# Inverse transform in four array quadrants, with a new order of pieces, in a spectral mixture-of-experts kernel

## The chip, the cores and the metric

The kernel runs on one core of a Trainium2 chip. The core has a matrix engine (TensorE, "PE" in the profile; its weight loads are shown as "PEld"), three engines for elementwise work (VectorE "DVE", ScalarE "ACT", GpSimd "POOL"), and a queue engine (SyncE "SP") that issues most transfers. TensorE writes into PSUM, an accumulator memory of eight banks; ACT and DVE move results from there to the on-chip memory SBUF. The metric is the device time of one execution in microseconds (us).

## The reference

The input x has 16 images of 64 channels and 128 x 128 pixels; all is float32. Two layers follow each other. The first:

```python
x_ht = dht_2d(x)                                   # 2-D Hartley transform
out_ht = zeros.at[:, :, :20, :20].set(compl_mul2d(x_ht[:, :, :20, :20], w1))
y = dht_2d(out_ht) / (H * W)
y = gaussian_smoothing_4d(y)                       # over all four axes
return y * (jnp.abs(fftfreq(W)) <= 0.25)           # only 65 of 128 columns stay
```

The second, on the result x of the first:

```python
residual = x
h = _afno(_group_norm(x, gn1_w, gn1_b), ...)       # 32 x 32 modes: MLP, inverse FFT
h = h + residual
residual = h
feats = _gelu(_c1(_group_norm(h, gn2_w, gn2_b), fe_w, fe_b))
shared = sum(_gelu(_c1(feats, shared_w[s], shared_b[s])) / 2 for s in range(2))
# gate: feats.mean -> small MLP -> scores of 16 experts; top 4, softmax
out = shared + sum(_gelu(_c1(feats, expert_w[e], expert_b[e])) * gate_w[:, e] for e in range(16))
return out + residual
```

An image is therefore the sum of two low-rank parts in the spectral domain, brought to pixels (one from the 32 x 32 modes of the second layer, one from the 20 x 20 modes of the first, the residual), then a channel mixing, then two shared and four chosen experts.

## The kernel before

**Three stages.** The first (lines up to 266) loads all of x and transforms it to 400 modes per image; the blur over images is folded into the sums `x2`. Between it and the second comes the modes stage (L288 to L321): 11 steps over `k1`, each of 40 fp32 matmul instructions into a PSUM tile `ps` that several copies take apart into `om` (ACT and DVE both on each tile), and a small product with `blurc` into `ot`. The second stage (L370 to L556) finds the group-norm statistics of the images from their modes, and runs the first MLP layer on 32 x 32 spectral points of each image (`spec` is its table of 3.2 MB); results go to device memory (`o1d`, and the 20 x 20 modes as `od` and `ond`).

**The mixture stage** (from L568) works on one image after the other, 16 in all, in pieces of fixed shape, each with a PSUM tile `pe` of two banks out of three such tiles:

- `spectrum` (L602): loads by the SP queue of the MLP values `s` and of the 20 x 20 modes into columns 64 and up of `bm`.
- `spectrum_f` (L613), two pieces: second MLP layer, 64 matmuls each, and one ACT copy (L629) into columns 0 to 63 of `bm`.
- `rows` (L635), eight tiles: transform along one image axis. Four matmuls per channel pair of 128 columns, in the four 64 x 64 quadrants of TensorE's array; ACT copies 105 partitions into `u` (L652). Partitions 0 to 63 of `u` hold the part of the 32 x 32 modes, 64 to 104 the residual's, and two more (105, 106) a bias term that `prepare` makes in the second stage and that reaches `u` through device memory (`b2x`).
- `pixels` (L658), eight tiles: the transform along the other axis, eight matmuls of 107 x 128 by 128 columns (both parts and the bias in one contraction). ACT evacuates with a bias into an `h` tile (L677), and DVE takes its statistics (L681, two per tile).
- `norm` (three steps), `feature` (eight tiles; L732, ACT's gelu L736) and `gate` (eight small steps, with four indirect loads of the chosen experts' weights on POOL, L806).
- `group`, 48 of them: an expert on a tile; four quadrant matmuls (L826), a gelu on ACT into one of the `g` tiles (L831), a weighted add into `h` on DVE (L834). The last expert of a tile is followed by its store.

A float32 matmul of the source is two instructions of TensorE, each with a weight load. On each engine instructions run in the order that was built. ACT evacuations are written one piece behind (`on_act`), DVE adds and statistics one more behind (`on_dve`).

**The order** of the pieces is written out by hand in `PIECES`: each piece has a list of positions, counted in groups of its own image (48 per image). Negative positions count back from the image's own group 0, so pieces of later images lie among the groups of the current one: -50 is two groups before group 0 of the image before it. Pieces are sorted by position, then by their place in the list.

Of the kernel before, what the change touches and what calls it, by code (L numbers as in the profile page):

```python
# [19 lines left out]
K = 20  # L20
# [10 lines left out]
KU = KC + 2  # L31
# [23 lines left out]
def constant_tables():  # L55
# [23 lines left out]
    inv1, inv2 = np.zeros((128, 2, N)), np.zeros((KU, N))  # L79
# [7 lines left out]
    inv2[KC], inv2[KC + 1] = inv2[:32].sum(0), inv2[32:64].sum(0)  # L87
    c, s = np.cos(a32).sum(0), np.sin(a32).sum(0)
    bias = np.array([[c, s], [-s, c]])

    by_half = lambda t: t.reshape(-1, 2, 2, N // 2).transpose(0, 1, 3, 2).reshape(-1, 2 * N)
    inv1, bias = by_half(inv1), by_half(bias)
# [38 lines left out]
    for loc in range(5):  # L131
# [13 lines left out]
        "bias": bias,  # L145
# [14 lines left out]
def hartley_afno_moe_kernel(ctx: ExitStack, tc: tile.TileContext, a: dict, out: bass.AP):  # L160
# [26 lines left out]
    with tc.tile_pool(name="modes", bufs=1) as mp:  # L187
# [6 lines left out]
        with tc.tile_pool(name="f_x", bufs=10) as xp, tc.tile_pool(name="f_t", bufs=2) as tp, \  # L194
# [9 lines left out]
            def along_columns(b, t1):  # L204
# [20 lines left out]
                for bo in range(NB):  # L225
                    g = float(gb[bo, b])
                    if g == 0.0:
                        continue
                    to = x2[:, 0, bo, :]
                    if bo in seen:  # L230
                        nc.vector.scalar_tensor_tensor(to, xf, g, to, ALU.mult, ALU.add)
                    else:
                        nc.vector.tensor_scalar(to, xf, g, None, ALU.mult)
                        seen.add(bo)
                    if not gb[bo, b + 1:].any():
                        nc.scalar.mul(x2[0:C, 1, bo], x2[C:P, 0, bo], -1.0)
                        nc.scalar.copy(x2[C:P, 1, bo], x2[0:C, 0, bo])
# [39 lines left out]
        spec = load(sc, "spec", [CH, 4, 2 * MD * MD])  # L277
        exw = load(sc, "exw", [P, C, NE])

        with tc.tile_pool(name="m_o", bufs=1) as op, \  # L280
# [7 lines left out]
            for k1 in range(K // 2 + 1):  # L288
# [9 lines left out]
                nc.scalar.copy(lok[:, k1], lo[:, :, 0])  # L298
                nc.vector.tensor_copy(upk[:, k1], up[:, :, 0])
                if k1 % (K // 2):  # L300
                    nc.scalar.copy(lok[:, K - k1, 0:1], lo[:, 0:1, 1])
                    nc.scalar.copy(lok[:, K - k1, K // 2 - 1:0:-1], lo[:, 1:, 1])
                    nc.vector.tensor_copy(upk[:, K - k1, ::-1], up[:, :, 1])
# [18 lines left out]


# [10 lines left out]
    b2 = kp.tile([2, C], F32, name="b2t")  # L334
    for ri in range(2):
        nc.sync.dma_start(b2[ri:ri + 1], a["b2"][32 * ri:32 * ri + 1, 0:C])
    bias = load(kp, "bias", [2, 2, N])
    b2r = kp.tile([P, 2, C], F32, name="b2r")
    b2x = dram.tile([2, N, C], F32, name="b2x")
    inv1 = load(kp, "inv1", [P, 2, N])  # L340
    inv2 = load(kp, "inv2", [KU, N])
# [20 lines left out]
    bm = kp.tile([P, CL, KC], F32, name="bm")  # L362
# [8 lines left out]
    with tc.tile_pool(name="s_w", bufs=2) as sw, tc.tile_pool(name="s_o", bufs=1) as so, \  # L371
# [134 lines left out]
        def prepare():  # L506
# [8 lines left out]
            ps = pp3.tile([P, 512], F32, name="pso")  # L515
            for i in range(2):
                nc.tensor.matmul(ps[:, i * C:(i + 1) * C], lhsT=bias[:, i], rhs=b2, start=True, stop=True)
            nc.scalar.copy(b2r.rearrange("p i c -> p (i c)"), ps[:, 0:2 * C])
            nc.sync.dma_start(b2x.rearrange("i n c -> n i c"), b2r)
# [50 lines left out]
    with s3:  # L570
        up_, hpp, fp, gp, selp = (pool(n, q) for n, q in (
            ("u", 1), ("hp", 14), ("feats", 9), ("g", 7), ("selw", 2)))
# [5 lines left out]
        nc.sync.dma_start(u[KC:KU], b2x)  # L578
# [22 lines left out]

        def spectrum(box):  # L602

            b = box["b"]
            s = box["s"] = sp.tile([P, MD * MD], F32, name="s")
            nc.sync.dma_start(s, o1d[b].rearrange("r c k -> (r c) k"))
            for h in range(2):
                r, i = (0, 32) if h else (64, 96)
# [4 lines left out]
        def spectrum_f(box, q):  # L613
# [13 lines left out]
            def evacuate():  # L627
                bmf = bm[:, :, 0:64].rearrange("p c (r j) -> p r c j", r=2)
                nc.scalar.copy(bmf[:, :, :, q * 16:(q + 1) * 16], ps.rearrange("p i r c -> p r c i"))  # L629
# [5 lines left out]
        def rows(box, q):  # L635


            if q == 0:
                if "spectrum" not in box:
                    flush()  # L640
            ps = ps2.tile([P, 2, 4, N], F32, name="pe")
            for i in range(4):
                for part, h in ((0, 0), (1, 0), (0, 1), (1, 1)):
                    k0 = C * (h ^ part)
                    rs = slice(k0, k0 + (HR if part else C))
                    cs = slice(64, KC) if part else slice(0, 64)
                    nc.tensor.matmul(ps[cs, h, i, :], lhsT=bm[rs, 4 * q + i, cs],  # L647
                                     rhs=inv1[rs, part], start=True, stop=True)

            def evacuate():  # L650
                dst = u[0:KC].rearrange("p n (h s) -> p h s n", h=2)[:, :, 4 * q:4 * q + 4, :]
                nc.scalar.copy(dst.rearrange("p h s n -> p n h s"),  # L652
                               ps[0:KC].rearrange("p h s n -> p n h s"))
# [4 lines left out]
        def pixels(box, t):  # L658
# [8 lines left out]
            for r in range(8):  # L667
                row = t * 8 + r
                nc.tensor.matmul(  # L669
                    ps[:, r // 4, r % 4 * N:(r % 4 + 1) * N],  # L670
                    lhsT=u[0:KU, 2 * row:2 * row + 2, :].rearrange("p h c -> p (h c)"),
                    rhs=inv2, start=True, stop=True)
# [190 lines left out]
        def step(name, make):  # L863
# [9 lines left out]
            (lambda box, i: spectrum(box), (-84,)),  # L873
            (spectrum_f, (-57, -50)),
            (feature, (-5, -4, -3, -2, -2, -2, -2, 0)),
            (step("norm", norm2), (-19, -16, -10)),
            (step("gate", gate), (2, 3, 5, 7, 8, 8, 10, 12)),
            (rows, (-50, -49, -48, -48, -48, -40, -39, -38)),
            (pixels, (-36, -32, -28, -24, -24, -24, -23, -23)),
# [80 lines left out]
```

## Time and profile before

| | us |
|---|---|
| median of 5 runs | 1856.02 (1853.68 to 1860.78) |
| the profiled execution | 1854.06 |
| its span, first to last instruction | 1852.0 |
| PE busy | 1696.2 (92%) |
| ACT busy | 1377.4 (74%) |
| DVE busy | 1270.6 (69%) |

By stage: the first takes 266 us and is filled by the load of x (the DMA engines are 90% and more busy until 200 us), the modes stage ends at 294 us, the second stage at 477 us, the first group starts at 532 us, and the mixture stage then repeats every 83 to 85 us. A "busy" TensorE counts matmuls with modelled ends, so 92% is not the share of its peak. In the lines, "<-" after an idle time names what ended it, and "issue" means that nothing in the profile did.

### The profile page before, as it was taken

The numbers are of one execution on the slowest core, as the hardware profiler recorded it, in microseconds if no ns is written. First come the engines' busy times: TensorE is split into PE (matmuls) and PEld (weight loads), VectorE is DVE, ScalarE is ACT, GpSimd is POOL, SyncE is SP. The second block draws the span as 40 slices with busy tenths as digits, with TensorE's granted clock in tenths as the row PEclk, the third lists the DMA queues.
The fourth block names the chain that finished last, engine by engine and source line by source line (L and its number), as shares of the span: only waits on it lengthen the run. The fifth ranks groups of instructions, "written<-read, shape, count | busy, mean of one in ns | idle before, by whom it ended". The sixth has DMA issues, their size and how long they took to land. (4 is left out here: it accounts for less than half of the span.)

```text
span 1852.0 us, 55817 instructions
## 1 busy us (share of the span) xinstructions
PE 1696.2 (92%) x24644; PEld 937.6 (51%) x24644; DVE 1270.6 (69%) x1774; ACT 1377.4 (74%) x1690; POOL 120.7 (7%) x140
## 2 busy tenths in 40 slices
PE   6677768999889999999999999999999999999996
PEld 5677764333645555454545455454545455554521
DVE  1233332322249788797979797887979797887988
ACT  2334343112478999989898989989898999989897
POOL 0000002003010101010110101010100101010110
PEclk9989989999999999999999999999999999999998
DMA  9989842114212222322232322322232322222023
GB/s 337 317 304 329 284 138 67 59 58 137 58 25 61 57 81 44 97 36 81 47 79 50 70 81 36 92 49 81 36 85 55 70 70 48 70 58 70 27 71 92
DMA packets 136129, 181.00 MB, mean 98 GB/s; under 512 B 94201, under 2 KB 95414, under 8 KB 135658
## 3 DMA queue, kind: packets, MB, share of 16 engines
q1 hardware_dynamic: 132192, 171.73, 33.0%
q0 software_dynamic: 3696, 5.71, 1.2%
q8 instruction: 193, 3.16, 0.7%
q14 instruction: 48, 0.39, 0.1%
HBM read 98.29 MB, written 79.11 MB: 96 GB/s over the span
## 5 line engine op out<-in xcount | busy, mean ns | idle before, releaser
L834 DVE SCALAR_TENSOR_TENSOR h<-g,wt,h 128x1024 f32<-128x1024 f32 x512 | 620.8, 1275 | 86.0 <-ACT g L831 86.0
L831 ACT ACTIVATE g<-pe,wl 128x1024 f32<-128x1024 f32 x512 | 540.0, 1128 | 9.4 <-PE pe L826 7.9
L826 PE MATMUL pe<-f,wl 64*64 64x512 f32 x4096 | 496.1, 600 | 2.1 <-DMA wl<-exd,ati 0.3
L834 DVE SCALAR_TENSOR_TENSOR h<-g,h 128x1024 f32<-128x1024 f32 x256 | 301.5, 1220 | 56.1 <-ACT g L831 56.1
L831 ACT ACTIVATE g<-pe,vec_sb 128x1024 f32<-128x1024 f32 x256 | 278.0, 1134 | 20.2 <-PE pe L826 20.1
L669 PEld LDWEIGHTS pe<-inv_sb,u 107*128 107x128 f32 x2048 | 234.4, 192 | 65.9 <-ACT g L831 35.1
L826 PEld LDWEIGHTS pe<-f,wl 64*64 64x64 f32 x4096 | 136.0, 132 | 238.5 <-ACT g L831 99.0
L669 PE MATMUL pe<-inv_sb,u 107*128 107x128 f32 x2048 | 248.8, 279 | 4.1 <-ACT g L831 2.8
L826 PE MATMUL pe<-f,shw 64*64 64x512 f32 x2048 | 251.2, 600 | 0.0
L677 ACT ACTIVATE h<-pe,gs 128x1024 f32<-128x1024 f32 x128 | 142.4, 1114 | 73.5 <-PE pe L669 61.3
L250 PE MATMUL ps<-fwd_sb,xt 128*64 128x64 f32 x4096 | 144.2, 234 | 56.3 <-issue 49.4
L681 DVE BATCH_NORM_STATS2 stats<-h 128x6 f32<-128x512 f32 x256 | 160.3, 679 | 27.1 <-ACT h L677 26.9
L250 PEld LDWEIGHTS ps<-fwd_sb,xt 128*64 128x64 f32 x4096 | 139.0, 150 | 59.8 <-issue 52.5
L647 PE MATMUL pe<-inv_sb,bm 64*64 64x128 f32 (+1 forms) x4096 | 143.4, 273 | 2.5 <-issue 2.5
L736 ACT ACTIVATE f<-pe,fb 128x1024 f32<-128x1024 f32 x128 | 144.1, 1136 | 1.7 <-PE pe L732 1.7
L253 ACT COPY t<-ps 128x320 f32<-128x320 f32 x128 | 53.3, 426 | 123.0 <-PE ps L250 122.8
L647 PEld LDWEIGHTS pe<-inv_sb,bm 64*64 64x64 f32 (+1 forms) x4096 | 117.0, 123 | 49.7 <-ACT f L736 24.5
L732 PE MATMUL pe<-h,fs 64*64 64x512 f32 x1024 | 133.1, 607 | 1.6 <-DVE n L709 1.6
L652 ACT COPY u<-pe 105x1024 f32<-105x1024 f32 x128 | 127.2, 1042 | 4.2 <-PE pe L647 3.2
L219 DVE TENSOR_TENSOR xm<-ps,pn 64x20 f32<-64x20 f32 x32 | 5.5, 171 | 177.4 <-ACT pn L215 177.2
L548 PE MATMUL psx<-spec_sb,ot 100*64 100x512 f32 x512 | 115.6, 594 | 0.0
L806 POOL DMA_INDIRECT wl<-exd,ati x64 | 66.8, 1044 | 696.8 <-ACT g L831 604.5
(164 smaller groups left out, 1153.7 us busy)
## 6 DMA issues: line engine op xcount, KB each, us to landing
xt<-in_x_dram SPq DMA_DIRECT2D x128, 512.0 KB
out_dram<-h SPq DMA_DIRECT2D x256, 256.0 KB
o1d<-o SPq DMA_DIRECT2D x16, 512.0 KB
s<-o1d SPq DMA_DIRECT2D x16, 512.0 KB
bm<-od SPq DMA_DIRECT2D x96, 50.0 KB
wk<-in_w_dram SPq DMA_DIRECT2D x11, 320.0 KB
wn<-in_w_dram SPq DMA_DIRECT2D x11, 320.0 KB
spec_sb<-in_spec_dram SPq DMA_DIRECT2D x1, 3200.0 KB
```

The lines of the kernel that those rows point to most:

```text
L250: nc.tensor.matmul(ps[cols, i, :], lhsT=xt[:, i, cols], rhs=fwd1, start=True, stop=True)
L548: nc.tensor.matmul(ps[ri * C:(ri + 1) * C], lhsT=ot[:, kc, b * C:(b + 1) * C], rhs=spec[:, kc, ri * 1024 + n * 512:ri * 1024 + (n + 1) * 512],
L647: nc.tensor.matmul(ps[cs, h, i, :], lhsT=bm[rs, 4 * q + i, cs], rhs=inv1[rs, part], start=True, stop=True)
L652: nc.scalar.copy(dst.rearrange("p h s n -> p n h s"), ps[0:KC].rearrange("p h s n -> p n h s"))
L669: nc.tensor.matmul(ps[:, r // 4, r % 4 * N:(r % 4 + 1) * N], lhsT=u[0:KU, 2 * row:2 * row + 2, :].rearrange("p h c -> p (h c)"), rhs=inv2, ...
L677: nc.scalar.activation(h, ps, AF.Identity, bias=gs1[:, 1, box["b"]:box["b"] + 1])
L681: nc.vector.bn_stats(box["stats"][:, 2 * t + p, :], h[:, p])
L732: nc.tensor.matmul(ps[p * C:(p + 1) * C, half], lhsT=box["fs"][rows_], rhs=box["h"][t][rows_, p], start=True, stop=True)
L736: nc.scalar.activation(f, ps, AF.Gelu, bias=box["fb"], accum_out=box["sums"][:, t:t + 1])
L826: nc.tensor.matmul(ps[half * C:(half + 1) * C, p], lhsT=w[rows_], rhs=f[rows_, half], start=True, stop=True)
L831: nc.scalar.activation(g, ps, AF.Gelu, bias=bias)
L834: nc.vector.scalar_tensor_tensor(h, g, share(), h, ALU.mult, ALU.add)
```

## The change

- Rows: each tile is 64 matmuls of 64 columns instead of 32 of 128, each quadrant filled. In `u`, partitions 0 to 63 are now one half of the pixels of an axis and 64 to 127 the other; the two parts (32 x 32 modes, residual) lie behind each other in columns.
- Pixels: per four image rows, four quadrant matmuls of 128 columns for the one part, then four that add the other part on the 66 columns that can be other than zero.
- The bias is no longer made in `prepare` and sent through device memory; it is added in the evacuation of `spectrum_f`, which is now two DVE operations of 512 elements a partition each instead of one ACT copy.
- `spectrum` is split: the load of `s` (`spectrum_in`) at -90, the loads of the modes at -74. The first `spectrum_f` piece is at -77 (behind the pixels of the image before), the second stays at -50. Rows, pixels, norm steps, features and gate steps have new positions.
- 16 instead of 14 `h` buffers, 8 instead of 7 `g` buffers; `bm` has 128 columns instead of 105.
- First stage: one of the two `x2` copies of an image is on DVE. Modes stage: all copies of a tile are on one engine, ACT and DVE in turn. The loads of `spec` and `exw` come after the modes stage.

```diff
-                        nc.scalar.copy(x2[C:P, 1, bo], x2[0:C, 0, bo])
+                        nc.vector.tensor_copy(x2[C:P, 1, bo], x2[0:C, 0, bo])
...
-        spec = load(sc, "spec", [CH, 4, 2 * MD * MD])
-        exw = load(sc, "exw", [P, C, NE])
...
-                nc.scalar.copy(lok[:, k1], lo[:, :, 0])
-                nc.vector.tensor_copy(upk[:, k1], up[:, :, 0])
+                copy = nc.vector.tensor_copy if k1 % 2 else nc.scalar.copy
+                copy(lok[:, k1], lo[:, :, 0])
+                copy(upk[:, k1], up[:, :, 0])
                 if k1 % (K // 2):
-                    nc.scalar.copy(lok[:, K - k1, 0:1], lo[:, 0:1, 1])
-                    nc.scalar.copy(lok[:, K - k1, K // 2 - 1:0:-1], lo[:, 1:, 1])
-                    nc.vector.tensor_copy(upk[:, K - k1, ::-1], up[:, :, 1])
+                    copy(lok[:, K - k1, 0:1], lo[:, 0:1, 1])
+                    copy(lok[:, K - k1, K // 2 - 1:0:-1], lo[:, 1:, 1])
+                    copy(upk[:, K - k1, ::-1], up[:, :, 1])
...
+    sc2 = on_modes.enter_context(tc.tile_pool(name="s_c2", bufs=1, side="right"))
+    spec = load(sc2, "spec", [CH, 4, 2 * MD * MD])
+    exw = load(sc2, "exw", [P, C, NE])
...
-            ps = pp3.tile([P, 512], F32, name="pso")
-            for i in range(2):
-                nc.tensor.matmul(ps[:, i * C:(i + 1) * C], lhsT=bias[:, i], rhs=b2, start=True, stop=True)
-            nc.scalar.copy(b2r.rearrange("p i c -> p (i c)"), ps[:, 0:2 * C])
-            nc.sync.dma_start(b2x.rearrange("i n c -> n i c"), b2r)
+            for r0 in (32, 96):
+                nc.scalar.mul(b2[r0:r0 + 32, 1], b2[r0:r0 + 32, 1], -1.0)
...
-            ("u", 1), ("hp", 14), ("feats", 9), ("g", 7), ("selw", 2)))
+            ("u", 1), ("hp", 16), ("feats", 9), ("g", 8), ("selw", 2)))
...
-        nc.sync.dma_start(u[KC:KU], b2x)
...
+        def spectrum_in(box):
+            s = box["s"] = sp.tile([P, MD * MD], F32, name="s")
+            nc.sync.dma_start(s, o1d[box["b"]].rearrange("r c k -> (r c) k"))
+
         def spectrum(box):
 
             b = box["b"]
-            s = box["s"] = sp.tile([P, MD * MD], F32, name="s")
-            nc.sync.dma_start(s, o1d[b].rearrange("r c k -> (r c) k"))
...
-                nc.scalar.copy(bmf[:, :, :, q * 16:(q + 1) * 16], ps.rearrange("p i r c -> p r c i"))
+                for i in (0, 8):
+                    j = q * 16 + i
+                    nc.vector.tensor_tensor(bmf[:, :, :, j:j + 8],
+                                            ps[:, i:i + 8].rearrange("p i r c -> p r c i"),
+                                            b2.unsqueeze(3).to_broadcast([P, 2, CL, 8]), ALU.add)
...
-            ps = ps2.tile([P, 2, 4, N], F32, name="pe")
+            ps = ps2.tile([P, 2, 4, 2, C], F32, name="pe")
             for i in range(4):
-                for part, h in ((0, 0), (1, 0), (0, 1), (1, 1)):
-                    k0 = C * (h ^ part)
-                    rs = slice(k0, k0 + (HR if part else C))
-                    cs = slice(64, KC) if part else slice(0, 64)
-                    nc.tensor.matmul(ps[cs, h, i, :], lhsT=bm[rs, 4 * q + i, cs],
-                                     rhs=inv1[rs, part], start=True, stop=True)
+                for part in range(2):
+                    for h, p in ((0, 0), (1, 1), (1, 0), (0, 1)):
+                        rs = slice(h * C, h * C + (HR if part else C))
+                        nc.tensor.matmul(ps[p * C:(p + 1) * C, h, i, part, :],
+                                         lhsT=bm[rs, 4 * q + i, part * C:(part + 1) * C],
+                                         rhs=inv1[rs, part, p * C:(p + 1) * C], start=True, stop=True)
...
-            for r in range(8):
-                row = t * 8 + r
-                nc.tensor.matmul(
-                    ps[:, r // 4, r % 4 * N:(r % 4 + 1) * N],
-                    lhsT=u[0:KU, 2 * row:2 * row + 2, :].rearrange("p h c -> p (h c)"),
-                    rhs=inv2, start=True, stop=True)
+            quadrants = ((0, 0), (1, 1), (0, 1), (1, 0))
+            for r in range(4):
+                n = 2 * (4 * t + r)
+                for p, half in quadrants:
+                    k = slice(p * C, (p + 1) * C)
+                    nc.tensor.matmul(ps[half * C:(half + 1) * C, p, r * N:(r + 1) * N],
+                                     lhsT=u[k, n + half, :], rhs=inv2[k, 0:N], start=True, stop=False)
+                for p, half in quadrants:
+                    k = slice(p * C, (p + 1) * C)
+                    to = ps[half * C:(half + 1) * C, p, r * N:(r + 1) * N]
+                    nc.tensor.matmul(bass.AP(to.tensor, to.offset, [to.ap[0], (N - MH, 2), (1, MH)]),
+                                     lhsT=u[k, C + n + half, :],
+                                     rhs=inv2[k, N:].rearrange("k (a n) -> k a n", a=2),
+                                     start=False, stop=True)
...
-            (lambda box, i: spectrum(box), (-84,)),
-            (spectrum_f, (-57, -50)),
-            (feature, (-5, -4, -3, -2, -2, -2, -2, 0)),
-            (step("norm", norm2), (-19, -16, -10)),
-            (step("gate", gate), (2, 3, 5, 7, 8, 8, 10, 12)),
-            (rows, (-50, -49, -48, -48, -48, -40, -39, -38)),
-            (pixels, (-36, -32, -28, -24, -24, -24, -23, -23)),
+            (lambda box, i: spectrum_in(box), (-90,)),
+            (lambda box, i: spectrum(box), (-74,)),
+            (spectrum_f, (-77, -50)),
+            (feature, (-8, -8, -4, -3, -3, -3, -3, -1)),
+            (step("norm", norm2), (-24, -21, -16)),
+            (step("gate", gate), (2, 3, 4, 5, 6, 7, 9, 11)),
+            (rows, (-48, -47, -45, -44, -43, -40, -39, -39)),
+            (pixels, (-34, -34, -33, -32, -31, -30, -30, -28)),
             (group, range(NG)),
```

## The prediction

> **What bounds the kernel now.** The page first: TensorE is busy for 92% of the span, and its code comes in 193 fetches: 3.16 MB for two instructions per matmul, so 64 bytes each and 256 to a fetch.
>
> ```profile
> span 1852.0 us, 55817 instructions
> PE 1696.2 (92%) x24644; PEld 937.6 (51%) x24644; DVE 1270.6 (69%) x1774; ACT 1377.4 (74%) x1690; POOL 120.7 (7%) x140
> q8 instruction: 193, 3.16, 0.7%
> ```
>
> Then busy times by window over one image of the mixture stage (gate to gate 83.3 to 84.9 us, mean 83.75). The columns are the stretch, then PE, PEld, DVE, ACT, POOL.
>
> ```profile
> 1031.50:1052.00 20.50, 19.09 (x308) 9.55 (x308) 14.82 (x24) 19.66 (x25) 0.32 (x1) 1.00 0.18 53
> 1052.00:1081.00 29.00, 28.76 (x248) 18.60 (x244) 27.17 (x33) 24.15 (x24) 4.66 (x5) 1.00 0.34 56
> 1081.00:1115.50 34.50, 33.74 (x562) 14.15 (x554) 28.35 (x33) 33.48 (x41) 0.56 (x1) 1.00 0.28 79
> ```
>
> ACT has almost no idle time in the first and third window, and 4.9 us in the second, that of the pixels: there it waits for TensorE. The timeline of TensorE shows the pace:
>
> ```profile
> 1069.77 5.63 PE L669 MATMUL pe<-inv_sb,u 107*128 107x128 f32 x48
> 1075.33 1.09 PE L826 MATMUL pe<-f,wl 64*64 64x512 f32 x8
> 1076.35 3.84 PE L669 MATMUL pe<-inv_sb,u 107*128 107x128 f32 x32
> ```
>
> and that of ACT in the same stretch, with the idle time and who ended it in brackets:
>
> ```profile
> 1073.65 1.11 ACT L677 ACTIVATE h<-pe,gs 128x1024 f32<-128x1024 f32 x1 [0.67 <-PE pe L669]
> 1075.43 1.11 ACT L677 ACTIVATE h<-pe,gs 128x1024 f32<-128x1024 f32 x1 [0.67 <-PE pe L669]
> ```
>
> A pixel tile takes 1.78 us (16 matmuls 0.1115 apart), a change between the 128x128 and the 64x64 mode 0.15 to 0.2 each way (1075.33 to 1076.35 is 1.02 for a group that takes 0.87 among others); ACT needs 1.00 for either. So ACT bounds most of the image, TensorE the pixels. VectorE is idle 13.4 us an image.
>
> Groups by line price the new parts (engine, operation, tiles, count | busy, mean ns | idle before), and two lines of TensorE's timeline at the first image show a wait with no engine behind it:
>
> ```profile
> L652 ACT COPY u<-pe 105x1024 f32<-105x1024 f32 x128 | 127.2, 1042 | 4.2 <-PE pe L647 3.2
> L629 ACT COPY bm<-pe 128x1024 f32<-128x1024 f32 x32 | 33.7, 1054 | 13.6 <-PE pe L622 13.3
> L483 DVE TENSOR_TENSOR ok<-psd,st 128x512 f32<-128x512 f32 x10 | 12.2, 1221 | 12.3 <-PE psd L480 12.3
> L681 DVE BATCH_NORM_STATS2 stats<-h 128x6 f32<-128x512 f32 x256 | 160.3, 679 | 27.1 <-ACT h L677 26.9
> ```
>
> ```profile
> 481.83 0.22 PE L622 MATMUL pe<-v2b,s 128*32 128x64 f32 x1 [1.57 <-issue]
> 488.23 0.52 PE L647 MATMUL pe<-inv_sb,bm 64*64 64x128 f32 x9 [1.28 <-issue]
> ```
>
> The last two are 256 TensorE instructions apart and follow no semaphore. 1.4 us before each, a packet of the code queue ended, and these packets never start closer than 3.3 us in the trace. I read: a block of 256 instructions can't be used up in less than some 3.4 us.
>
> **The change part by part.** Per image, in start-to-start times.
>
> *Pixels.* A tile becomes 64 matmuls in four quadrants: four rows, each of two sets 128 wide and two 66 wide. Sets 128 wide run 0.109 apart in the rows stage (L647, four quadrants at once). For 66 wide no row exists: pairs 64 wide (L212) start 0.0584 apart, so 0.060; the upper bound is 0.109, if a weight load or the strided output holds them to the wider pace. Tile: 4 x (0.219 + 0.120) = 1.36, with ramp 1.40 (bound 1.80). No mode change is left.
>
> *Rows.* 64 matmuls of 64 columns instead of 32 of 128: 16 sets x 0.0584 = 0.93 for 0.88 now. ACT's 0.92 per tile stays (same 1024 elements a partition), and ACT bounds there: nothing. If that cover went, 8 x 0.05 = 0.4.
>
> *Evacuating the spectrum.* ACT loses 2 x 1.05 = 2.1. VectorE gets four tensor_tensor of 512. Bounds 0.69 (L440, same size, contiguous) and 1.22 (L483, scattered output); runs of eight lie between: 0.95, so 3.8 of its 13.4 idle. Behind them on VectorE are adds and statistics, for which ACT waits only when the eight g buffers are full: from the end of a g to the start of its add the lag grows to 4.5 us before the features today; later to perhaps 7, of 8 x 1.15 = 9. What it can cost is the PSUM buffer, one of three, held until VectorE comes, and rows that wait for bm; behind the features the lag is near 0 (10 us idle there today), and two groups and a feature lie between.
>
> *Order.* The pixels move from 14 groups to 7 (groups 14 to 20, with a spectrum piece). TensorE there: 8 x 1.40 + 7 x 0.87 + 2.2 for the piece (1.92 and mode changes) = 19.5. Code: 8 x 128 + 256 + 112 = 1392 instructions, 5.4 blocks, 18.5 us at 3.4: mostly hidden, but two tiles, a group and the piece in a row are 528 instructions in 5.9 us, where 7 are needed: 1.0. Less 0.5 that TensorE is ahead of ACT at its start: 20.0. ACT has 15 us of work there: 5.0 idle, for 6.2 today (28.2 us from group 11 to 25 for 22 of work).
> The second spectrum piece, among the features: ACT had its own copy (1.05) to fill TensorE's 2 us; now it idles 1.0. So half of the 2.1 comes back as a wait. Norm steps come 4, 3 and 5 groups after what they need (4, 3 and 6 now) and wait on VectorE's lag: 0.9 (1.0 now). Features come 8 groups after the last norm step instead of 5; the eighth still waits for group 46 to free its f buffer. Gate steps stand one group and mostly one row apart, where two groups or none stood; ACT's work lies between either way: 0. Rows behind the second piece, code: 0.4.
> ACT work 48 x 1.00 + 8 x (0.92 + 1.00 + 1.09) + 2.35 (gate, its waits, norm) = 74.4; with idle 5.0 + 1.0 + 0.9 + 0.4 the period is 81.7, so -2.05. Fifteen images' stretches: -31. Bounds: stretch 18 (no code stall) to 23.2 (66-wide sets at 0.109): -4.1 to +1.2 each, -62 to +18.
>
> *Queues.* SP: the s load and eight spectrum loads go from group 12 to 6 and 22; they land within 6.5 us and are needed 13 and 26 groups later. The store and load through b2x go, and two small matmuls and a copy in `prepare`, off the path; so does a 64 KB load ahead of the first pixels. POOL: gathers one group earlier, used from group 16; its memset of bm grows by a fifth, unawaited. hp with 16 buffers ends ACT's wait for stores (7.5 us in all, inside the stretches counted).
>
> *First image.* Two pieces, eight rows, eight pixels without groups, so code bounds: rows 8 x 1.7 = 13.6 for 10.6, pixels 13.6 for 14.5, a piece among them +1.4, two VectorE evacuations +0.4, other waits -1.4: +2.5 (-5 to +6).
>
> *Modes stage.* 27.8 us for 11 steps. Today ACT and VectorE take turns on one tile (four copies of 0.41 to 0.46, a small one, 0.53 idle at each turn: 2.05 a step), and TensorE twice stood 3 us beside the load of spec. Then whole tiles alternate: (1.2 + 1.85 + 0.4) / 2 = 1.7 a step, 19.8 in all: -8. The spec load (23 us) starts after it and lands some 8 us before its first use; its effect on code fetches moves with it to a stretch where TensorE is busy 30.3 of 31.2: +4. Net -4 (-11 to +4).
> *x2 copies.* The last five pairs on ACT (0.54 each) split over two engines: -1.3 (-2.7 to +1).
>
> Sum, against the profiled execution's 1854.06: -31 + 2.5 - 4 - 1.3 = 1820. That execution lies 2 us under the median of the runs: 1822.
>
> **A rule weighed.** The Trainium skill (Runtime: NRT & Kernel Launch, Instruction fetch mechanics) says that TensorE holds 2048 instructions and that crossing a block of 256 is mostly hidden. The idle 1.57 and 1.28 us above say otherwise. By the page the 1.4 us a period and 8 in the first image would go: some 1793.
>
> **The rivals.**
> *Code bounds (slower).* TensorE's instructions per image go from 2300 to 3500. Before 488.23 a fetch came 3 us late beside a 512 KB load. The pixel stretch has 5.4 blocks; it reaches today's share of idle time at 22 us, so at 4.1 us a block. At 4.5 it takes 24.3, 4.3 more than forecast: 81.7 + 4.3 = 86.0, 2.3 above today's, 15 x 2.3 + 5 for the first image = 40 over 1856: 1895. Against: steady-state packets take 1.0 us, and loads were put apart from the dense places.
> *Quadrants slow (slower).* 66-wide sets at 0.109: 3.2 more than forecast each period, 1822 + 48 = 1870. Against: pairs of L212 load 64 columns each in 0.0584.
> *VectorE's lag sets the norm steps (no change).* Evacuations at 1.22 and the pixels' statistics bunched put the lag near 4 at the first norm step; it and the next then wait 1 us each: +1.9 a period on the forecast, 1850. For: today a norm step already waits 1.1 us on it.
> *Fetch hidden.* The change gives all its TensorE time: 1793.
>
> **How the numbers follow.** Forecast (1803 to 1843) 0.46; fetch hidden 0.20; VectorE's lag 0.12; code bounds 0.15; quadrants slow 0.07. A difference under 0.2% (3.7 us) can't be told from none. Faster 0.46 + 0.20 + half of 0.12 = 0.72; same 0.05; slower 0.23. The range leaves out most of code-bound and the best of hidden fetch: 1783 to 1869.
>
> **What would show it.** Pixel tiles 1.35 to 1.45 us apart where two follow each other; ACT idle near 1 us beside the second piece; no mode change around pixels; period near 81.7. The first image's rows at 1.7 a tile with idle "issue" before TensorE. Idle "issue" inside the pixel stretch above 3 us an image, or 66-wide sets near 0.109, would make me wrong upwards; none at all, downwards.

## The result: no measurable change

The changed kernel takes 1853.3 us (median; 1847.5 to 1858.7), the kernel before 1853.8 beside it: a ratio of 0.9997 with a 95% interval of 0.9989 to 1.0005. The forecast was 1822, a ratio of 0.982. The profiled execution's span is 1851.7 us for 1852.0. Its page, first lines and four groups (busy, mean ns | idle before, who ended it):

```profile
span 1851.7 us, 76281 instructions
PE 1665.8 (90%) x34880; PEld 902.1 (49%) x34880; DVE 1323.3 (71%) x1859; ACT 1340.1 (72%) x1638; POOL 124.1 (7%) x140
...
q8 instruction: 274, 4.49, 1.0%
...
L842 ACT ACTIVATE g<-pe,wl 128x1024 f32<-128x1024 f32 x512 | 543.1, 1157 | 62.7 <-PE pe L837 60.9
L837 PE MATMUL pe<-f,wl 64*64 64x512 f32 x4096 | 513.3, 603 | 17.6 <-DVE bm L629 11.2
...
L688 ACT ACTIVATE h<-pe,gs 128x1024 f32<-128x1024 f32 x128 | 142.6, 1115 | 42.0 <-PE pe L680 37.3
...
L655 ACT COPY u<-pe 128x1024 f32<-128x1024 f32 x128 | 128.8, 1012 | 34.3 <-PE pe L649 28.6
```

ACT lost the 34 us of the spectrum's copies (1377 to 1340 busy) and finished no sooner: it waits 62.7 us before expert groups and 34.3 before rows. The second group names a waiter that the kernel before did not have: TensorE stands before a group until VectorE has emptied bm's tile (L629).

The same image as three windows of the prediction showed, now in the changed kernel (stretch, PE, PEld, DVE, ACT, POOL busy; clock, DMA share, GB/s): groups 0 to 13, the pixels, and the experts behind them.

```profile
1204.07:1227.20 23.13, 21.66 (x583) 11.76 (x575) 15.04 (x27) 21.19 (x26) 4.37 (x5) 1.00 0.31 59
1227.20:1248.14 20.94, 19.58 (x670) 16.10 (x673) 20.94 (x27) 16.19 (x16) 0.61 (x1) 1.00 0.05 10
1248.14:1267.58 19.44, 19.06 (x166) 5.89 (x158) 18.62 (x25) 19.25 (x21) 0.56 (x1) 1.00 0.27 73
```

In the pixels VectorE is busy for all of 20.94 us. Before the change it had 1.8 idle in 29.

Where the time went, from the two profiled executions (ACT's first group of the mixture starts at 533.7 before, 539.3 after): up to the first group +5.6 (forecast -2.8: modes -4, x2 copies -1.3, first image +2.5); the fifteen image periods 1250.3 to 1243.3, -7.0 (forecast -31); the last image +1.1. That is -0.3. Per image, ACT's start to start, mean over images 3 to 13 (the forecast's column adds up its own terms: 14 groups, 8 rows at 0.92, 2.2 for the gate and 0.4 of code in the first line, and so on):

| groups | forecast | after |
|---|---|---|
| 0-13, rows and gate | 24.0 | 24.4 |
| 14-20, pixels and first piece | 20.0 | 20.7 |
| 21-39, experts and norm steps | 20.0 | 19.5 |
| 40-45, features | 13.6 | 13.6 |
| 46-47, second piece | 4.1 | 5.1 |
| period (83.9 before) | 81.7 | 83.2 |

### The profile page after: what moved, and what is told of

It reads as the page before. It is cut to its first block, busy times and chain, and to the rows that moved or that the text cites. A ratio compares the mean times of both kernels' runs of the same rounds, so it can differ in the third digit from the quotient of the medians.

```text
span 1851.7 us, 76281 instructions
## 1 busy us (share of the span) xinstructions
PE 1665.8 (90%) x34880; PEld 902.1 (49%) x34880; DVE 1323.3 (71%) x1859; ACT 1340.1 (72%) x1638; POOL 124.1 (7%) x140
## 5 line engine op out<-in xcount | busy, mean ns | idle before, releaser
L842 ACT ACTIVATE g<-pe,wl 128x1024 f32<-128x1024 f32 x512 | 543.1, 1157 | 62.7 <-PE pe L837 60.9
L837 PE MATMUL pe<-f,wl 64*64 64x512 f32 x4096 | 513.3, 603 | 17.6 <-DVE bm L629 11.2
L837 PE MATMUL pe<-f,shw 64*64 64x512 f32 x2048 | 264.5, 595 | 1.8 <-ACT u L655 1.7
L675 PE MATMUL pe<-inv_sb,u 64*64 64x128 f32 x4096 | 197.2, 271 | 10.0 <-issue 8.8
L675 PEld LDWEIGHTS pe<-inv_sb,u 64*64 64x64 f32 x4096 | 169.3, 134 | 54.5 <-issue 40.0
L248 PE MATMUL ps<-fwd_sb,xt 128*64 128x64 f32 x4096 | 138.0, 228 | 57.1 <-issue 48.7
L680 PE MATMUL pe<-inv_sb,u 64*64 64x66 f32 x4096 | 180.3, 218 | 6.0 <-issue 5.6
L680 PEld LDWEIGHTS pe<-inv_sb,u 64*64 64x64 f32 x4096 | 169.1, 133 | 5.1 <-issue 5.1
L248 PEld LDWEIGHTS ps<-fwd_sb,xt 128*64 128x64 f32 x4096 | 132.1, 143 | 61.2 <-issue 52.5
L649 PE MATMUL pe<-inv_sb,bm 64*64 64x64 f32 (+1 forms) x8192 | 149.2, 221 | 9.2 <-issue 8.5
L649 PEld LDWEIGHTS pe<-inv_sb,bm 64*64 64x64 f32 (+1 forms) x8192 | 139.5, 135 | 36.5 <-issue 26.4
L655 ACT COPY u<-pe 128x1024 f32<-128x1024 f32 x128 | 128.8, 1012 | 34.3 <-PE pe L649 28.6
```

What stands on the lines that cost most here:

```text
L248: nc.tensor.matmul(ps[cols, i, :], lhsT=xt[:, i, cols], rhs=fwd1, start=True, stop=True)
L649: nc.tensor.matmul(ps[p * C:(p + 1) * C, h, i, part, :], lhsT=bm[rs, 4 * q + i, part * C:(part + 1) * C], rhs=inv1[rs, part, p * C:(p + 1) ...
L655: nc.scalar.copy(dst.rearrange("p h s n -> p n h s"), ps.rearrange("p h s a n -> p (a n) h s"))
L675: nc.tensor.matmul(ps[half * C:(half + 1) * C, p, r * N:(r + 1) * N], lhsT=u[k, n + half, :], rhs=inv2[k, 0:N], start=True, stop=False)
L680: nc.tensor.matmul(bass.AP(to.tensor, to.offset, [to.ap[0], (N - MH, 2), (1, MH)]), lhsT=u[k, C + n + half, :], rhs=inv2[k, N:].rearrange( ...
L837: nc.tensor.matmul(ps[half * C:(half + 1) * C, p], lhsT=w[rows_], rhs=f[rows_, half], start=True, stop=True)
```

## The experiments

All ratios are to the kernel before. "Hold" is the time from a piece's last matmul to the end of its evacuation.

### Who empties the spectrum's PSUM tile

Four runs: ACT's copy put back, with the bias left out (act_spectrum); the old order; code shortened, with the real pixels left out; and the one edit made in the kernel before.

```diff
 act_spectrum
-                for i in (0, 8):
-                    j = q * 16 + i
-                    nc.vector.tensor_tensor(bmf[:, :, :, j:j + 8], ... b2 ..., ALU.add)
+                nc.scalar.copy(bmf[:, :, :, q * 16:(q + 1) * 16], ps.rearrange("p i r c -> p r c i"))
 old_places: the eight lists of PIECES from the kernel before; spectrum_in and spectrum at -84
 short_code
-            for r in range(4):
+            for r in range(3):
...
+                    c0 = r % 2 * 256
+                    nc.tensor.matmul(ps[half * C:(half + 1) * C, p, c0:c0 + 256],
+                                     lhsT=u[k, n + half, :], rhs=inv1[k].rearrange("k a n -> k (a n)"), ...)
 before_dve
-                nc.scalar.copy(bmf[:, :, :, q * 16:(q + 1) * 16], ps.rearrange("p i r c -> p r c i"))
+                nc.vector.tensor_copy(bmf[:, :, :, q * 16:(q + 1) * 16], ps.rearrange("p i r c -> p r c i"))
```

> The spectrum pieces are evacuated by one copy on ACT again; the bias b2 is left out. Theory P (as predicted: the move to VectorE is worth 2.1 us of ACT's time an image, of which 1.0 comes back as waiting): period +1.1, 1866 to 1872. Theory L (ACT waits for TensorE beside a piece whoever empties it: 2.0 idle beside the second piece, 2.0 beside the first): the copies fill idle time, period -0.5 to +0.3, 1845 to 1857, ACT's idle before the group behind the second piece falls from 1.0 to below 0.5.

> The parts of the change with the order of before (pixels over 14 groups, both pieces and the last features where they were). Theory L: what costs is dense TensorE work in few groups. Pixels of 1.34 in 14 groups need 8 x 1.34 + 14 x 0.87 = 22.9 of TensorE for 22 of ACT, so 23.5 to 24.5 with the bunch at the end, for 28.2 before the change; the pieces cost 2.0 each beside features: period 80 to 81.5, 1805 to 1828, faster than both. Theory F agrees within 1 us a period (five tiles and two groups in a row are 672 instructions, 2.6 blocks, 9.7 us for 8.4). Theory O (the order is what makes the new parts pay: gathers and gate are disturbed by dense work): period at or above 83.2, 1853 or more.

> Leaves out the real pixels: a tile becomes 24 matmuls, 256 columns wide (the rows' table as right side), instead of 64, so TensorE's stream stays (6 pairs at twice 0.109 = 1.31 us, for 1.34) and its code falls from 128 to 48 instructions a tile. Pixel stretch, groups 14 to 20: 20.7 us in the changed kernel. Theory F (code: blocks of 256 instructions 3.4 to 4.0 us apart bound the stretch): 752 instructions are 2.9 blocks, 11 us, so the stream alone counts: 18.8, -1.9 a period; the first image's rows and pixels -4; in all about -32, 1821 us. Theory L (the stream itself, with three PSUM tiles of lead, bounds it): stretch 20.2 to 20.7, period unchanged within 0.4, only the first image's -4: 1845 to 1850.

> The kernel before, with one edit: VectorE instead of ACT copies the two spectrum pieces out of PSUM. ACT's work falls by 2.1 us an image. Theory P (the prediction's step): period -1.0, 1840. Theory V: both pieces stand where VectorE's queue is long (groups 39 and 46); in old_places the first was held 5.6 us and TensorE stood 3.8 beside it. Hold 4 to 6 at the first piece, 2 to 3 at the second, period +2 to +5 over 83.8: 1885 to 1930.

| kernel | emptied by | hold, 1st / 2nd piece | TensorE idle beside | period | time, ratio |
|---|---|---|---|---|---|
| before | ACT | 1.1 / 1.1 | 0 / 0 | 83.9 | |
| after | VectorE | 2.8 / 2.6 | 0.4 / 0.8 | 83.2 | 1853, 0.9997 |
| act_spectrum | ACT | 1.1 / 1.1 | 0.3 / 0 | 81.2 | 1827, 0.987 (0.983-0.992) |
| old_places | VectorE | 5.6 / 2.6 | 3.8 / 0.8 | 91.6 | 1973, 1.064 (1.061-1.068) |
| before_dve | VectorE | 6.6 / 2.5 | 4.8 / 0.7 | 90.6 | 1957, 1.053 (1.051-1.056) |
| short_code | VectorE | 5.1 / 2.6 | 2.9 / 0.8 | 83.8 | 1856, 1.000 (0.998-1.002) |

before_dve takes 2.1 us an image from ACT and gives back 6.7. Its timelines of TensorE, VectorE and ACT around one first piece:

```profile
965.51 1.95 PE L826 MATMUL pe<-f,wl 64*64 64x512 f32 x16
972.22 3.69 PE L826 MATMUL pe<-f,wl 64*64 64x512 f32 x16 [4.76 <-DVE bm L629]
```

```profile
968.56 2.47 DVE L834 SCALAR_TENSOR_TENSOR h<-g,wt,h 128x1024 f32<-128x1024 f32 x2
970.95 1.22 DVE L629 COPY bm<-pe 128x1024 f32<-128x1024 f32 x1
```

```profile
974.27 1.11 ACT L831 ACTIVATE g<-pe,wl 128x1024 f32<-128x1024 f32 x1 [5.49 <-PE pe L826]
```

The piece is followed by two groups (965.51), and the third needs the piece's own buffer, because three PSUM tiles go round in order. VectorE still has adds in front of the copy, so TensorE stands 4.76 and ACT 5.49 us. The changed kernel shows the same in small at its second piece (TensorE, then VectorE):

```profile
1282.35 1.09 PE L837 MATMUL pe<-f,wl 64*64 64x512 f32 x8
1283.26 1.04 PE L743 MATMUL pe<-h,fs 64*64 64x512 f32 x8
1285.14 1.09 PE L837 MATMUL pe<-f,wl 64*64 64x512 f32 x8 [0.84 <-DVE bm L629]
```

```profile
1282.51 1.28 DVE L845 SCALAR_TENSOR_TENSOR h<-g,wt,h 128x1024 f32<-128x1024 f32 x1 [0.92 <-ACT g L842]
1283.71 1.28 DVE L629 TENSOR_TENSOR bm<-pe,b2t 128x512 f32<-128x512 f32 x2
```

Here VectorE was even idle until 1282.51; one add in front and its own 1.28 make the hold 2.6, which is more than the 1.8 that two tiles give TensorE to do. With ACT's copy groups 46 and 47 take 4.5 instead of 5.1, the copy included. The page of act_spectrum has 20.5 us in the place of the 62.7:

```profile
L838 ACT ACTIVATE g<-pe,wl 128x1024 f32<-128x1024 f32 x512 | 543.9, 1158 | 20.5 <-PE pe L833 18.4
```

Theory P falls. Theory L's time for act_spectrum (1845 to 1857) missed too, by 18 us and more, and my expectation for old_places had the sign wrong: its pixels did cost less, but the first piece stood at group 39 among the experts, and a norm step at group 29 waited 4.2 us for VectorE. short_code speaks against the code: with 48 instructions a tile instead of 128, groups 14 to 18 fell from 14.5 to 13.0, and groups 19 and 20 rose from 6.2 to 8.3, because VectorE was still behind when the first piece came (held for 5.1 us instead of 2.8). Some 1.0 of the 1.5 gained is not code: this run lacks a long first pixel tile that the changed kernel has (see below), as hold_loads does, with 13.4.

### Is the code a bound?

short_act joins short_code and act_spectrum. rows_wide gives the rows other matmuls:

```diff
 rows_wide
-                        nc.tensor.matmul(ps[p * C:(p + 1) * C, h, i, part, :], ...
-                                         rhs=inv1[rs, part, p * C:(p + 1) * C], start=True, stop=True)
+                    for h, p in ((0, 0), (1, 1), (1, 0), (0, 1))[2 * part:2 * part + 2]:
...
+                        (twice) nc.tensor.matmul(ps[p * C:(p + 1) * C, h, i].rearrange("k a n -> k (a n)"),
+                                         lhsT=bm[rs, 4 * q + i, p * C:(p + 1) * C], rhs=inv1[rs, part], ...)
```

> short_code and act_spectrum together (leaves out the real pixels and the bias). In short_code the pixels got faster by 1.3 us (groups 14 to 19) and 2.5 were lost again at group 20, where TensorE stood 2.9 us while VectorE held the piece's PSUM tile for 5.1. With that hold gone, theory F (code has a share in the pixel stretch): groups 14 to 20 in 17.5 to 18.3 for 19.6 in act_spectrum, period 79 to 80, 1795 to 1812. If code has none there: 19.2 to 19.7, period 80.7 to 81.2, and only the first image's gain of some 6 us, 1818 to 1824.

> Leaves out the real rows: a tile becomes 32 matmuls 128 columns wide, the shape that the kernel before used, instead of 64 of 64 columns; TensorE's stream is 0.88 for 0.93 us and its code half. First image's rows took 16.8 us in the changed kernel (10.6 before the change), with 6.2 idle without a semaphore. Theory F (code bounds the first image's rows, 2.1 us a tile): 9.5 to 11 for the eight, -6; in the period at most -0.5; 1838 to 1848. If the rows' form is not it: 1850 to 1857.

short_act: 1819.5, 0.981 (0.978-0.984); its period is 81.15 for 81.24 in act_spectrum. Groups 14 to 20 gained 1.1 (18.5 for 19.6, between the two theories), and rows and norm steps lost 1.0. Code costs a us in the pixels and next to nothing in the period.

rows_wide is not what its expectation describes: its instructions stayed as many, and by their order two quadrants ran at a time, so that a tile took 1.75 us and not 0.88 (1926.5, 1.038). It still tells something. In the first image, twice the stream (14.0 us for eight tiles) moved the eight rows only from 16.8 to 17.8 us. What bounds them there shows in TensorE's timeline of the changed kernel:

```profile
481.98 2.15 PE L649 MATMUL pe<-inv_sb,bm 64*64 64x64 f32 x97 [1.44 <-issue]
485.98 2.54 PE L649 MATMUL pe<-inv_sb,bm 64*64 64x64 f32 x128 [1.85 <-issue]
489.72 6.17 PE L649 MATMUL pe<-inv_sb,bm 64*64 64x64 f32 x256 [1.19 <-issue]
496.91 0.69 PE L649 MATMUL pe<-inv_sb,bm 64*64 64x64 f32 x31 [1.02 <-issue]
498.75 0.45 PE L675 MATMUL pe<-inv_sb,u 64*64 64x128 f32 x8 [1.15 <-ACT u L655]
```

Each matmul stands for two instructions, so x128 is a block of 256. TensorE stops without a semaphore at the blocks' ends, and the code queue's packets start 3.3 to 4.1 us apart here; so I read code as the bound. The kernel before, with half the instructions for nearly the same stream (0.88 for 0.93 a tile), took 10.6. From 485.98 to 496.91 three blocks take 3.6 us each, where I had 3.4. The rest of the 16.8 us is 4.0 for the first 194 instructions and 1.8 for the last 62, of which 1.15 is a wait for ACT's last copy into `u`. The Trainium skill (Runtime: NRT & Kernel Launch, Instruction fetch mechanics) calls a block's crossing mostly hidden; the periods of short_act and act_spectrum agree with it, the first image does not.

### The held tile, or VectorE's work?

bias_dve keeps VectorE's work and takes it off PSUM: ACT copies, VectorE adds the bias in SBUF. bias_pool gives that add to GpSimd. tuned1 moves the pieces away from the features.

```diff
 bias_dve (bias_pool: nc.gpsimd)
+                nc.scalar.copy(bmf[:, :, :, q * 16:(q + 1) * 16], ps.rearrange("p i r c -> p r c i"))
+                half = bmf[:, :, :, q * 16:(q + 1) * 16]
+                nc.vector.tensor_tensor(half, half, b2.unsqueeze(3).to_broadcast([P, 2, CL, 16]), ALU.add)
 tuned1: bias_dve, and
+            (spectrum_f, (-74, -63)),
+            (step("norm", norm2), (-25, -22, -14)),
+            (step("gate", gate), (1, 2, 3, 5, 6, 7, 10, 14)),
+            (rows, (-51, -48, -48, -41, -40, -38, -37, -35)),
+            (pixels, (-33, -32, -32, -31, -30, -29, -28, -28)),
```

> The changed kernel with the spectrum pieces copied out of PSUM by ACT and the bias added afterwards by VectorE, in place in SBUF. VectorE does as much work as in the changed kernel (2 x 1.2 us an image), but no PSUM tile waits for it. Theory V (a PSUM tile held until VectorE's queue comes to it stops TensorE two tiles later: 2.6 and 2.8 us of hold in the changed kernel, 5.6 with the old places): hold 1.1, period 81.0 to 82.0, 1825 to 1842. Rival (it was VectorE's extra work, not the held tile, that act_spectrum took away): period 82.8 to 83.5, 1846 to 1858.

> As bias_dve, with the add on GpSimd, which is idle 93% of the span. Theory V: as act_spectrum, 1824 to 1834, if the add (no GpSimd add of this size is in the traces; a fill of the larger tile took 3.4 us) is done before the rows, 2 groups behind the second piece; each us that it is later than that delays the rows. Rival: GpSimd's add slows VectorE's work beside it, and its gathers come later: 1845 or more.

> bias_dve with other places: the pieces at groups 22 and 33, behind the pixels, and no piece among the features; rows a little looser, the last norm step two groups later. Adding up the work in order with the measured pitches gives 3 us a period less than bias_dve: period 78 to 79.5, 1785 to 1805. If dense TensorE work among the expert groups costs as much as among features: 81 to 82, as bias_dve.

bias_dve: 1846.1, 0.9958 (0.9941-0.9976). The hold is gone (1.1 and 1.1), and of the 23 us between act_spectrum and the changed kernel (0.987 and 0.9997) only 7 came; the period of 82.9 lies in the rival's range, not in theory V's. So theory V is a part of it; VectorE's work in that place is another. The clearest pair is hold_bias_dve (below) beside act_spectrum. Its VectorE has two adds of 1.22 us an image more (and a small one that holds loads), and groups 21 to 39 take 21.2 for 20.0: ACT waits 0.9 at group 24 and 0.9 at 27 (0.05 and 0.7 in act_spectrum), where TensorE's norm steps wait for VectorE. Who waited for whom, first in hold_bias_dve, then in act_spectrum (us in total, times, longest):

```profile
PE pa L707 <- DVE mv L695: 22.2, 16, 3.2
PE pa L715 <- DVE n L712: 13.6, 15, 0.9
```

```profile
PE pa L703 <- DVE mv L691: 7.7, 5, 3.2
PE pa L711 <- DVE n L708: 12.1, 15, 0.9
```

The changed kernel beside act_spectrum alone doesn't separate these causes: half of their 2.0 us a period lies in groups 14 to 18 (14.5 and 13.5), where the changed kernel has a long first pixel tile (two sections below) and act_spectrum hasn't. hold_loads and hold_bias_dve have the short tile as well. Their periods are 83.4, with VectorE emptying the PSUM tile, and 82.4, with ACT emptying it and VectorE adding in SBUF; act_spectrum's is 81.2, without the add. So with the short tile the hold costs 1.0 us a period and VectorE's work some 1.2 (with the small instruction that holds the loads). In the changed kernel the long tile overlaps with them: taking away the hold alone gives 0.4 there (82.9 in bias_dve), and taking away the long tile alone gives nothing (83.4 in hold_loads).

bias_pool: 1859.6, 1.004 (1.002-1.006). GpSimd's add takes 1.95 us, and the rows waited for it (idle 0.5 before group 0 and 1.1 before group 9, for 0 and 0.1 in act_spectrum). tuned1: 1856.7, 1.001 (0.999-1.004), with a period of 83.9 above both of its ranges: the second piece among the experts cost only 1.3 instead of 1.4, but ACT waited 2.3 us at group 13, beside the last rows, which my adding up had missed.

### The load beside the modes

```diff
 spec_late: a VectorE memset of one column of spec behind the modes' copies; the load behind all other loads
 spec_gate
+            nc.scalar.mul(spec[0:C, 0, 0:1], om[0][0:C, 15, K // 2:K // 2 + 1], 0.0)
+            nc.scalar.mul(spec[C:CH, 0, 0:1], om[1][C:CH, 15, K // 2:K // 2 + 1], 0.0)
+            nc.scalar.dma_start(spec, a["spec"].rearrange("p (a b) -> p a b", a=4))
```

> The load of spec (3200 KB) and exw truly start behind the modes: spec waits for a VectorE instruction after the last of the modes' copies, and both stand last among the loads. In the changed kernel the spec load still ran beside the modes stage, which took 29.4 us with two idle spells of TensorE of 4.5 and 3.2 us. If the load beside the code fetches makes these spells: 20 to 23 us for the stage, -6 to -9 in all (1844 to 1848), unless the same spells come back beside the load in the next stage (0). If the spells are the fetch's own: 28 to 30 us, 1850 to 1856.

> The changed kernel with the load of spec held by data: one element of it is first written by ACT from the last of the modes' results, and the load is issued by ACT's queue. In spec_late the instruction that was to hold it needed no such data and ran ahead (266.1), so the load left at 269.1, beside the modes as before. Theory C (the load beside the modes delays the code): TensorE's two spells of 4.5 and 3.2 us go, stage 29.4 to 21 or 22; the load then runs beside the next stage until 318, with at most 2 spells there: -4 to -8, 1845 to 1849. Theory N: stage 28 to 30, 1850 to 1858.

spec_late: 1857.8, 1.001 (0.999-1.003), and a miss: the memset needs no data, ran at 266.1, and the load left at 269.1. That is also what the change does: its load leaves at 266.23, and that of the kernel before left at 265.75. In the changed kernel's timeline of SP's queue the moved load leaves before the modes have well begun (264), and TensorE stands twice beside it:

```profile
266.23 0.37 SPq L170 DMA_DIRECT2D spec_sb<-in_spec_dram  x1
```

```profile
281.76 1.96 PE L290 MATMUL psm<-x,wk 128*64 128x64 f32 x42 [4.28 <-issue]
...
291.53 1.27 PE L290 MATMUL psm<-x,wk 128*64 128x64 f32 x36 [2.95 <-issue]
```

In spec_gate, where it waits for data, the stage runs without them:

```profile
275.21 2.56 PE L292 MATMUL psm<-x,wk 128*64 128x64 f32 x80 [1.17 <-DVE om L303]
278.68 2.56 PE L292 MATMUL psm<-x,wk 128*64 128x64 f32 x80 [0.91 <-DVE om L303]
282.15 2.58 PE L292 MATMUL psm<-x,wk 128*64 128x64 f32 x80 [0.91 <-DVE om L303]
```

From its first matmul to the next stage's takes 20.6 us instead of 29.4, and the mixture's first group starts 5.9 us earlier. All four runs with this edit have a stage of 20.6 to 21.0 us; the other runs with the changed kernel's modes stage have 26.0 to 30.5. The time of spec_gate alone, 1850.5, 0.999 (0.996-1.002), can't be told from none, and together with bias_dve (below) the interval still overlaps that of bias_dve.

### A long first pixel tile, not settled

In the changed kernel's profiled execution the first pixel tile takes 2.6 to 3.2 us in 11 of 15 images, 1.35 is due. I suspected the eight spectrum loads: they stand at group 22 in the order, but left behind group 9, as soon as the rows had read bm, beside the gathers.

```diff
 hold_loads (hold_bias_dve: the same in bias_dve; after_again: nothing)
+            if b:
+                nc.vector.tensor_scalar(bm[:, 0, 64:KC], boxes[b - 1]["h"][-1][:, 0, 0:KC - 64], 0.0, None, ALU.mult)
```

> The changed kernel with the eight spectrum loads truly held back: they wait for a VectorE instruction (41 zeros, made from the last pixel tile) that stands at their place in the order, group 22. In the changed kernel they left at group 9, as soon as the rows had read bm, beside the gathers and the first pixel tile: share of the DMA engines 0.85 to 0.9 for 5 us, and TensorE stood 1 to 1.8 us inside the first pixel tile in 11 of 15 images without a semaphore (1.16 us of ACT's idle time in group 14, mean). Theory C (code arrives late beside these 5300 small packets): group 14 from 4.4 to 3.2 us, period 82.0, 1834 to 1842. Theory N (the loads have no part in it): 83.2, 1848 to 1856.

> bias_dve with the spectrum loads held back as in hold_loads. bias_dve kept the same stand in the first pixel tile (1.17 in group 14), which act_spectrum did not show. Theory C: period 82.9 to 81.6, 1822 to 1832. Theory N: 1843 to 1850.

> The changed kernel, unaltered. If the long first pixel tile belongs to the kernel (its code, its order, its loads): again 2 to 3.2 us in most images and group 14 near 4.4 us. If it belongs to the execution: 1.35 and 3.2, with group 20 at 4.2 to 4.6 instead of 3.0, since VectorE then comes later to the first piece; in both cases 1848 to 1857.

hold_loads: the tile took 1.35 us, but the time was 1858.6, 1.002 (0.999-1.004): groups 14 to 18 fell from 14.5 to 13.4, groups 19 and 20 rose from 6.2 to 7.7, hold 4.1 at the first piece. And the loads are not the cause: spec_late, whose loads were where they had been, has 1.35 too, and all_three (below), whose loads were held, has the long one (up to 3.2). after_again (1854.2) has the long tile again, so it belongs to the program as built; what in it, no run tells. hold_bias_dve: 1845.4, 0.996 (0.994-0.999), no better than bias_dve: what the short tile gained came back at the norm steps.

### Taken together

```diff
 all_three: bias_dve, hold_loads, spec_gate, and
+            (step("norm", norm2), (-22, -18, -14)),
 both: bias_dve and spec_gate
 both_norm: both, and
+            (step("norm", norm2), (-23, -19, -13)),
```

> The changed kernel with bias_dve (ACT empties the pieces), hold_loads, spec_gate, and the norm steps 2, 3 and 2 groups later, since in hold_bias_dve ACT waited 0.9 at groups 24 and 27 while TensorE's norm steps waited for VectorE. If these are the losses: modes and start -6 (spec_gate), period 82.2 to 80.5 or 81.3; 1815 to 1830, the predicted time. If a fourth bound takes over (the last norm step close before the features, or VectorE's work as a whole): period 82 or more, 1838 to 1845.

> The changed kernel with bias_dve's and spec_gate's edits together, the order untouched. They act in different stages, so the sum: -8 and -4 to -5 under the changed kernel's 1853: 1839 to 1843. If the start's gain is given back in the first image: 1845 to 1848.

> As both, with the norm steps at groups 25, 29 and 35 instead of 24, 27 and 32. In hold_bias_dve ACT lost 1.0 and 1.0 at groups 24 and 27, in all_three (26, 30, 34) 0, 0.1 and 2.8. If the waits are VectorE's lag behind each step, four groups suffice for the second and six for the third: -1 to -2 a period, 1812 to 1828. If the third step still waits: 1840 to 1850.

all_three: 1878.3, 1.011 (1.009-1.013), slower than both of its theories. Its third norm step, four groups behind the second, made ACT wait 1.9 us at group 34 and 0.6 in the next two. both: 1840.7, 0.993 (0.990-0.995), in line with the sum of its parts. both_norm: 1833.2, 0.990 (0.986-0.993), between its two ranges, and faster than the kernel before and the changed one by 1%. The norm steps no longer stop ACT (groups 21 to 39 take 19.2), and its page has:

```profile
span 1831.7 us, 76298 instructions
...
L843 ACT ACTIVATE g<-pe,wl 128x1024 f32<-128x1024 f32 x512 | 544.3, 1184 | 6.5 <-PE pe L838 4.7
```

Its period is still 82.3, with the long first tile in it, and its first image no shorter than the changed kernel's.

## Why the prediction was wrong, step by step

**The step that failed** is "Evacuating the spectrum". I set VectorE's four operations against "3.8 of its 13.4 idle" an image, and priced the PSUM buffer "held until VectorE comes" at nothing behind the features. Their size was overstated (0.61 apart, 0.68 the last one; I took 0.95). The place was what failed. VectorE's idle time lies beside the rows (15.0 busy of 23.1), where no piece is; in the pixels, where the first piece went, it has none. And "two groups and a feature lie between" is the wrong count: with three tiles in rotation TensorE stops after two. Where the first pixel tile is short, this costs 2.2 us an image (1.0 for the held tile, 1.2 for VectorE's work: hold_loads, hold_bias_dve, act_spectrum); the period missed by 1.5. In the changed kernel itself the long tile, whose cause is open, hides a part of it. That act_spectrum's 81.2 lies near the forecast's 81.7 confirms nothing: it leaves out the bias, and ACT makes the copies that the forecast had taken from it. The Trainium skill (TensorEngine Tiling (Array Packing), PSUM Bottleneck) advises to use both ScalarE and VectorE to empty PSUM. Here emptying these tiles with VectorE cost time in both kernels: 7 us in the changed one (1853.3 for bias_dve's 1846.1), 13 with the short first tile (hold_loads' 1858.6 for hold_bias_dve's 1845.4), and 101 in the one before (1957 for 1855).

**Second piece among the features**: the forecast had 1.0 us of ACT's time lost, and 2.0 were (5.1 us for 3.1 of work). **Pixels**: the tile was right (1.34 for 1.40; sets 66 wide stand 0.058 apart), and the stretch took 20.7 for 20.0. **Rows**: a tile took 0.93, as forecast. **Code in the period**: the 1.0 us in the stretch is there, as short_act shows, but it was worth nothing net. **Norm steps**: they cost 0.4 for 0.9. They had more room, because TensorE was late; once it was not, they cost the 0.9 and more (hold_bias_dve).

**First image**: from the first piece to TensorE's first group it took +7.5 (55.2 to 62.7) for +2.5, beyond its range of -5 to +6. The rows took 16.8 for 13.6: "8 x 1.7" had a block of 3.4 us where 3.6 were measured, no late first block (4.0 for three quarters of one) and no wait for ACT's last copy (1.15). Rows, piece and pixels together cost 9 more than before, and the features behind gave 1.3 back.

**Modes stage**: forecast 19.8 for the steps alone, and 20.6 is what spec_gate shows. What fell is "The spec load starts after it". Its place in the program held nothing back, and the stage took 29.4 instead of 27.8. The +4 for the stretch behind the modes was too much: with the load truly there, in spec_gate, that stretch takes 183.2 for 182.0. **x2 copies**: this term was right, 4.7 us from the last sum to the modes for 6.1. **Queues**: this was the same error. The eight loads that "go from group 12 to 6 and 22" left behind group 9; it cost nothing that the runs show.

**The rivals.** "VectorE's lag" came nearest: no change, 1850. It had the right engine, but the number was luck: it put +1.9 a period on the norm steps, and in the changed kernel these cost less than forecast. They stopped ACT for longer only where the tile was no longer held (0.9 twice in hold_bias_dve). "Code bounds" fits the first image alone. "Quadrants slow" and "fetch hidden" are out. I had given VectorE's lag one place to act, and it had two.

## What to carry to other kernels

Work moved to an engine with idle time on average is free only if the idle time is where the work is put, and if nothing short waits behind that engine's queue: here a PSUM tile in a rotation of three allowed two tiles of delay, 1.8 us, and the hold was 2.6. Read the busy time of the receiving engine in that window, and count tiles, not microseconds on average. In these runs a transfer started when its data and its buffer were ready, wherever it stood in the program (`spec` at 266 us, the spectrum loads behind group 9); what held it back was an operand that was late (spec_gate).

## What I had not expected of the hardware and its queues

Beside a 3200 KB load TensorE stood 4.28 and 2.95 us without a semaphore, and with the load moved away it didn't: 8.8 us of that stage. Time gained in front of a full queue came back, and more: short_code, spec_late and hold_loads, all without the long first pixel tile, have groups 14 to 18 faster by 1.0 to 1.5 us than the changed kernel, and groups 19 and 20 slower by 1.5 to 2.1. That tile of 2.6 to 3.2 us, which some builds have and others, equal in that place, have not, stays without a cause.
